# Graph attention over 2708 nodes: the last node tile's weights in four groups, and one division per block of four head pairs

## The chip, the cores and the metric

One core of one Trainium2 chip runs the whole program in one launch. The metric is the device time of an execution in microseconds (us), the median of several runs. A profile is one further execution, recorded by the hardware profiler, with its own time. TensorE is PE in the profile (its weight loads are PEld), VectorE is DVE, ScalarE is ACT, GpSimd is POOL, and SP issues most of the DMA transfers.

## The reference

Four graph layers work on x (2708 nodes, 512 features) and a 2708 x 2708 adjacency matrix; each is followed by a residual sum and a layer norm. Layers 0 and 1 are sums over neighbours, and the last stage is an attention with one head and a two-layer MLP. The change lies in the two attentions with eight heads of 64 features (layer 2, and the first half of layer 3), of this form:

```python
Wh = jnp.einsum('ni,hio->hno', h, W)
a1, a2 = (a[:, :OUT_F], a[:, OUT_F:])
f1 = jnp.einsum('hno,ho->hn', Wh, a1)
f2 = jnp.einsum('hno,ho->hn', Wh, a2)
e = jax.nn.leaky_relu(f1[:, :, None] + f2[:, None, :], ALPHA)
masked = jnp.where(adj[None] > 0, e, NEG_INF)
attention = jax.nn.softmax(masked, axis=-1)
h_prime = jnp.einsum('hnm,hmo->hno', attention, Wh)
```

## The kernel before, in words

**Tiles.** The nodes make NT = 22 tiles of P = 128 rows; the last tile (LAST) has only `few` = 20. The transposed mask `maskT` holds neighbours m on the partitions and nodes n on the columns. The columns are cut into two blocks of 11 tiles, 1408 and 1300 columns wide.

**Weights.** Up to factors that are applied elsewhere, the weight of neighbour m for node n is max(v[n], u[m]) times the mask, with v and u exponentials of the two projections f1 and f2. `Weights.weights` computes it for one neighbour tile j, one head and a whole block of columns in one DVE instruction, e (line 743). `Weights.load` broadcasts the head's row v to all partitions by DMA, `v_bc`. The column u of tile j is `ucol[:, j, h]`.

**Products and divisors.** PE multiplies e with R2, the projected features scaled by `ecol`, and sums over the tiles j into the PSUM tiles `po`, up to 512 columns each; the two heads of a pair use the two halves of PE's columns (line 937). For the softmax's divisor, `Weights.above` lets ACT compute c, which tells where u was above v (a steep sigmoid into 8 bits, line 770); PE multiplies c with the narrow columns `parts_c` into `pd` (`divisors`, line 839), and the mask with `parts_m` (`masks`, line 822). Each of these is a number split into three bf16 parts. `fold` adds the parts up by small matmuls (line 811), and `divide` makes reciprocals of the sums in `rcs` (lines 861 to 866).

**Order.** `heads_attention` goes through 8 runs per layer (two blocks, four head pairs each). In a run the 22 tiles j come in the order 0 to 9, LAST, 10 to 20, and at each tile the two heads' e, c and products. Steps that are left over from the run before are hung on positions of the order in `todo`: the rest of the divisors at 0, `fold` at 4, `divide` at 6, and in layer 2 turning the result (`turn`, `store`) at 8, 9, 12, 13, 16, 17. `keep` copies the mask's share of the divisors at position 2 of a block's first run. There are five buffers for e and three for `v_bc`. Each engine takes its instructions in one order that is fixed when the program is compiled.

**The last tile.** Its 20 neighbours would leave most partitions idle. So both heads of a pair share one e: rows 0 to 31 belong to the first head, rows 32 on to the second (TWIN = 32). `load_both` loads v for both (line 752), into the buffer that also holds the projection's weights, one run ahead. The mask rows of LAST lie four times on the partitions, at 0, 32, 64 and 96; the later two copies are made by two SP DMAs at line 585. In R2, `ecol` and `ucol` the rows of a head are zero for the other head.

**Projection.** `project` makes Wh for all tiles, with f1 and f2 as further columns of the same matmuls. On LAST with eight heads (`twice`) it copies the tile's 20 columns to a second place, and takes exponentials and scaled products head by head parity (lines 676 to 681). On the first block's and the last tile it splits `ecol` and the product of `ucol` and `ecol` into bf16 parts on DVE (`split`). The first few e's of an attention are computed while its projection still runs (`first`, `many` = 5 and 4), so that the attention's sixth e is the first that has to wait for a buffer. The sigmoids and the exponentials need different tables in ACT.

**After.** Layer 2's result goes to `o_dram` by SP; the next projection loads it through SP (`summed`). Layer 3's result goes to `oT_dram` and its reciprocals through `spread` to `rc_dram`, and the last projection loads both through SP (`elu_turned`).

Of the kernel before, what the change touches and what calls it, by code (L numbers as in the profile page):

```python
# [9 lines left out]
F32 = mybir.dt.float32  # L10
# [20 lines left out]
def kernel(  # L31
# [545 lines left out]
    for g in range(4):  # L577
        rows_m = ident[:, 32 * g:32 * g + 3 * H].rearrange("p (h i) -> p h i", i=3)
        rows_c = ident[:, 32 * g:32 * g + 12].rearrange("p (k q i) -> p k q i", k=2, q=2)
        nc.vector.tensor_reduce(pick_m[:, g], rows_m, AX.X, OP.add)  # L580
        nc.vector.tensor_reduce(pick_c[:, g], rows_c, AX.X, OP.add)


    for g in (2, 3):
        nc.sync.dma_start(maskT[g * TWIN:g * TWIN + few, LAST, :N], maskT[:few, LAST, :N])
# [20 lines left out]
    def project(name, source, layer, v_dram, cuts, turned=None, first=None):  # L606
# [12 lines left out]
        with ExitStack() as ph:  # L619
# [24 lines left out]
            for t in range(NT):  # L644
# [7 lines left out]
                twice = heads > 1 and t == LAST  # L652
                if twice:
                    nc.gpsimd.memset(xT[:, :, n:TWIN], 0.0)
                    nc.gpsimd.tensor_copy(xT[:, :, TWIN:TWIN + n], xT[:, :, :n])
                elif t == LAST:
                    for g in range(1, 4):
                        nc.gpsimd.memset(xT[:, :, g * TWIN - TWIN + n:g * TWIN], 0.0)
                        nc.gpsimd.tensor_copy(xT[:, :, g * TWIN:g * TWIN + n], xT[:, :, :n])
                m = n if t < LAST else TWIN + n if twice else 3 * TWIN + n  # L660
# [11 lines left out]
                if twice:  # L672
                    for k in range(2):
                        at = slice(k * TWIN, k * TWIN + n)
                        d2 = pm[1][at, D // 2 + k:D // 2 + heads:2]
                        nc.scalar.activation(ecol[at, t, k::2], d2, AF.Exp, scale=ALPHA)
                        for i in range(2):
                            nc.scalar.activation(ucol[at, t, i::2], d2, AF.Exp, scale=1.0 - ALPHA)
                        for a in range(2):
                            view = lambda y: y.rearrange("p (h k o) -> p h k o", k=2, o=HO)[:, :, k]  # L680
                            nc.vector.tensor_mul(view(R2[at, t, a * D // 2:(a + 1) * D // 2]), view(pm[a][at, :D // 2]),
                                                 ecol[at, t, a * hh + k:(a + 1) * hh:2, None].to_broadcast([n, hh // 2, HO]))
                else:
                    d2 = d if m == n else pm[1][:m, D // 2:D // 2 + heads]
                    nc.scalar.activation(ecol[:m, t, :heads], d2, AF.Exp, scale=ALPHA)
                    nc.scalar.activation(ucol[:m, t, :heads], d2, AF.Exp, scale=1.0 - ALPHA)
                with tc.issue_after(scaled[t - 1].ins) if first and t else nullcontext():
                    made = first(t) if first else None
                for a in range(0 if twice else 2):
                    to, src = R2[:m, t, a * D // 2:(a + 1) * D // 2], pm[a][:m, :D // 2]  # L690
                    if heads > 1:
                        with tc.issue_after(made.ins) if made else nullcontext():
                            scaled[t] = nc.vector.tensor_mul(to.rearrange("p (h o) -> p h o", h=hh),
                                                             src.rearrange("p (h o) -> p h o", h=hh),
                                                             ecol[:n, t, a * hh:(a + 1) * hh, None].to_broadcast([n, hh, HO]))
                    else:
                        scaled[t] = nc.scalar.activation(to, src, AF.Copy, scale=ecol[:m, t, 0:1])
                if heads > 1:
                    nc.scalar.activation(vcol[:n, t, :], b[:n, :], AF.Exp, scale=ALPHA - 1.0)
                    nc.gpsimd.tensor_scalar(bcol[:m, t, :], ucol[:m, t, :], -STEP * (1.0 + 2.0 ** -22), None,  # L700
                                            op0=OP.mult)
                a, z = next(c for c in cuts if c[0] <= t < c[1])
                if t == z - 1:
                    if heads > 1:
# [7 lines left out]
                        if z == NT:  # L712

                            nc.vector.tensor_copy(pairs_c[:, LAST, :, 0, 6:12], pairs_c[:, LAST, :, 1, 6:12])
# [8 lines left out]
    class Weights:  # L723
# [16 lines left out]
        def weights(self, b, h, j, v):  # L740
            c0, w = self.blocks[b][0] * P, self.width(b)
# [5 lines left out]
        def load_both(self, b, h0):  # L747
# [3 lines left out]
            for h, a, z in ((h0, 0, TWIN), (h0 + 1, TWIN, P)):  # L751
                nc.sync.dma_start(v[a:z, :w], self.v_dram[h, c0:c0 + w].partition_broadcast(z - a))
# [738 lines left out]
```

## Time and profile before

| what | us |
|---|---|
| median of 3 runs | 2942.97 (2942.67 to 2946.18) |
| the profiled execution | 2939.28 |
| its span, first to last instruction | 2937.5 |
| layers 0 and 1, to the first attention's projection | 858 |
| projection of layer 2 | 858.0 to 949.8 |
| attention of layer 2 | 949.8 to 1493.0 |
| projection of layer 3 | 1493.0 to 1596.0 |
| attention of layer 3 | 1596.0 to 2140.0 |
| last projection, last attention, MLP | 2140.0 to 2937.5 |

Over the whole span PE is busy 97%, PEld 54%, DVE 68%, ACT 52% and POOL 7%, and the granted TensorE clock is 0.995. A share of the whole span hides that the stages have different limits, so the busy times are best read stage by stage, and then the waits: the engine that others wait for sets the pace. A matmul's end is modelled in the profile, so a busy PE is not a PE at its peak. A fp32 matmul is recorded as two instructions.

### The profile page before, as it was taken

To read this page: it belongs to the slowest core of one execution; us is meant where nothing else is said; L and a number is where in the kernel's file an instruction comes from. 1 tells how busy PE (TensorE), PEld (TensorE's weight loads), DVE (VectorE), ACT (ScalarE), POOL (GpSimd) and SP (SyncE) were. 2 spreads that over 40 slices of the span, in tenths; PEclk is the share of its full clock that TensorE was granted. 3 is DMA by queue.
4 is the path that set the end of the run, shared out by engine and by line. 5 is a ranking of instruction groups with operands and counts; after the bars stand their busy time and mean duration, and the time that the engine had idled before them with its cause. 6 is when DMAs were issued, how large, how long until landed. Compare 5 with 4: busy or idle time off the path is not lost. (4 is left out here: it accounts for less than half of the span.)

```text
span 2937.5 us, 36437 instructions
## 1 busy us (share of the span) xinstructions
PE 2854.5 (97%) x14354; PEld 1590.3 (54%) x14354; DVE 1996.9 (68%) x2409; ACT 1515.0 (52%) x1761; POOL 220.2 (7%) x375
## 2 busy tenths in 40 slices
PE   8999999999999999999999999999999999999997
PEld 4557766458887333444466433444475555555555
DVE  6866637443234999999977999999953435445242
ACT  3546532123323999999965999999951000000001
POOL 1111101101110000000022000000000000000000
PEclk9999999999999999999999999999999999999999
DMA  5633326322222011111143111121061000000000
GB/s 131 129 87 76 104 79 192 113 67 91 81 74 82 30 40 39 38 45 48 32 151 123 40 40 39 43 64 37 33 158 61 4 26 15 25 15 16 15 22 21
DMA packets 121886, 185.71 MB, mean 63 GB/s; under 512 B 42455, under 2 KB 67276, under 8 KB 121706
## 3 DMA queue, kind: packets, MB, share of 16 engines
q1 hardware_dynamic: 91838, 121.62, 13.8%
q0 software_dynamic: 18864, 57.45, 6.9%
q10 hardware_dynamic: 11004, 4.22, 0.6%
q8 instruction: 115, 1.88, 0.3%
q14 instruction: 65, 0.53, 0.1%
HBM read 153.10 MB, written 44.65 MB: 67 GB/s over the span
## 5 line engine op out<-in xcount | busy, mean ns | idle before, releaser
L743 DVE SCALAR_TENSOR_TENSOR e<-v_bc,ucol,maskT 128x1408 f32<-128x1408 f32 (+3 forms) x804 | 1135.9, 1468 | 326.9 <-PE pn L1119 313.4
L770 ACT ACTIVATE c<-e,bcol 128x1300 fp8e4<-128x1300 f32 (+1 forms) x688 | 965.5, 1422 | 65.3 <-DVE e L743 22.3
L937 PE MATMUL po<-e,R 128*64 128x512 f32 (+2 forms) x4224 | 907.5, 549 | 30.4 <-DVE e L743 27.4
L937 PEld LDWEIGHTS po<-e,R 128*64 128x64 f32 x4224 | 341.9, 137 | 563.0 <-issue 386.1
L1119 PE MATMUL pn<-e,R 128*128 128x512 f32 (+3 forms) x1056 | 403.0, 545 | 1.1 <-DVE lin L1139 0.3
L1119 PEld LDWEIGHTS pn<-e,R 128*128 128x128 f32 (+1 forms) x1056 | 183.9, 190 | 197.1 <-issue 181.5
L1069 ACT ACTIVATE w<-pl,b 128x256 f32<-128x256 f32 (+1 forms) x88 | 41.0, 466 | 371.2 <-PE pl L1067 371.2
L496 PE MATMUL acc<-yH,kT 128*128 128x512 f32 x484 | 195.2, 409 | 4.6 <-ACT kT L369 4.5
L547 PE MATMUL acc<-yH,mf 128*128 128x512 f32 x484 | 185.0, 389 | 0.0
L496 PE MATMUL acc<-yL,kT 128*128 128x512 f32 x462 | 180.7, 391 | 0.0
L547 PE MATMUL acc<-yL,mf 128*128 128x512 f32 x462 | 179.7, 389 | 0.0
L663 PE MATMUL pm<-w,xT 128*128 128x264 f32 (+1 forms) x704 | 165.3, 387 | 2.0 <-ACT xT L135 1.1
L259 PE MATMUL pm<-weight,xT 128*128 128x512 f32 (+1 forms) x344 | 158.4, 603 | 8.1 <-DVE u L352 6.8
L1067 PE MATMUL pl<-lin 128*128 128x256 f32 (+1 forms) x704 | 156.1, 376 | 3.4 <-DVE lin L966 3.4
L122 POOL TENSOR_TENSOR ln_rs<-ln_rs,half 128x1 f32<-128x1 f32 (+1 forms) x88 | 53.5, 608 | 1407.7 <-DVE ln_rs L121 1358.2
L1092 PE MATMUL pl<-lin,w 128*128 128x512 f32 x336 | 150.8, 593 | 0.0
L1067 PEld LDWEIGHTS pl<-lin 128*128 128x128 f32 x704 | 131.3, 193 | 34.6 <-issue 15.8
L544 ACT CAST mf<-maskT 128x1024 fp32r<-128x1024 fp8e4 (+1 forms) x66 | 64.5, 978 | 151.7 <-PE acc L547 148.1
L663 PEld LDWEIGHTS pm<-w,xT 128*128 128x128 f32 (+1 forms) x704 | 127.9, 187 | 26.2 <-issue 2.9
L259 PE MATMUL pm<-w,xT 128*128 128x512 f32 x296 | 133.6, 594 | 5.3 <-ACT xT L135 2.1
L369 ACT ACTIVATE kT<-maskT 128x512 fp32r<-128x512 fp8e4 (+1 forms) x132 | 77.5, 594 | 115.5 <-PE acc L496 114.3
L839 PE MATMUL pd<-c,parts_c 128*12 128x384 fp8e4 (+2 forms) x2752 | 128.3, 307 | 0.0
(247 smaller groups left out, 2643.2 us busy)
## 6 DMA issues: line engine op xcount, KB each, us to landing
rows<-x_dram SPq DMA_DIRECT2D x63, 256.0 KB
v_bc<-v_dram SPq DMA_DIRECT2D x16, 704.0 KB
rows<-in_x_dram SPq DMA_DIRECT2D x42, 256.0 KB
x_dram<-u POOLq DMA_DIRECT2D x42, 256.0 KB, 2.6
v_bc<-v_dram SPq DMA_DIRECT2D x16, 650.0 KB
m<-in_adj_dram POOLq DMA_DIRECT2D x13, 677.0 KB, 7.0
r_dram<-u POOLq DMA_DIRECT2D x21, 256.0 KB, 2.4
rows<-r_dram SPq DMA_DIRECT2D x21, 256.0 KB
```

The costliest lines, as they stand in the source:

```text
L259: order(nc.tensor.matmul(pm[:m], xT[:, k, :m], w[:, k, :], start=(k == 0), stop=(k == KD - 1)))
L369: made = nc.scalar.activation(kT[:, :w], maskT[:, j, b[0] * P:b[0] * P + w], AF.Relu, scale=-1.0)
L496: nc.tensor.matmul(pa[t], kT[:, (t - b[0]) * P:(t - b[0] + 1) * P], y[:, j, :], start=(j == 0 and y is yH), stop=(j == LAST))
L547: nc.tensor.matmul(pa, mf[:, j - g0, :], y[:, j, :], start=(j == 0 and y is yH), stop=(j == LAST))
L663: nc.tensor.matmul(pm[a][:m, :D // 2 + heads], xT[:, k, :m], w[:, k, a, :D // 2 + heads], start=(k == 0), stop=(k == KD - 1))
L743: self.made = nc.vector.scalar_tensor_tensor(e[:, :w], v[:, :w], ucol[:, j, h:h + 1], maskT[:, j, c0:c0 + w], op0=OP.max, op1=OP.mult)
L770: nc.scalar.activation(c[:, :w], e[:, :w], AF.Sigmoid, bias=bcol[:, j, h:h + 1], scale=STEP, saturate=False)
L839: pe(nc.tensor.matmul(p[32 * g:32 * g + 12, :c1 - c0], parts_c[:, j, h, :], c[:, c0:c1], start=(i == 0 and h == hs[0]), stop=(i == NT - 1 ...
L937: pe(nc.tensor.matmul(po[i][HO * k:HO * k + HO, :c1 - c0], R2[:, j, h * HO:(h + 1) * HO], e[:, c0:c1], start=(i_ == 0), stop=(i_ == NT - 1)))
L1067: nc.tensor.matmul(pl[:, :w], self.lin1[:, k, f * P:(f + 1) * P], h[:, k, :w], start=(k == 0), stop=(k == KD - 1))
L1092: nc.tensor.matmul(pl[:n], gT[:, f, (t - t0) * P:(t - t0) * P + n], self.lin2[:, f, :], start=(f == 0), stop=(f == KF - 1))
L1119: nc.tensor.matmul(pn[k][:, :w], R2[at, j, k * P:(k + 1) * P], e[at, :w], start=(j == 0), stop=(j == NT - 1))
```

## The change

Three things are done.

First, LAST's weights in the head attentions are made for four groups of 32 rows: two heads by two segments of the block's columns. The second segment begins 512 columns (SEG) after the first, so an e holds 896 columns (or 788) in place of 1408 (or 1300). PE takes the product of each head and column part from the 32 rows of its group. `load_both` issues four DMAs, one for each group. The mask rows of the third and fourth group are shifted by 512 columns, and set back before the last projection (`last_rows`). The projection copies LAST to all four groups, treats all heads at once, and zeroes what does not belong to a group by a product with `sel` and by a copy within `ucol`.

Second, the sums of a block's four pairs are folded into one PSUM tile, `sums`, where they stay; `divide` runs once per block for all eight heads, with four instructions in place of five, and `keep` is gone. The buffers of `ps_t` go from two to one to make room in PSUM.

Third, what follows from this: divisors of LAST are cut at the segment's border, and the last projection uses the same copies as the others.

```diff
-    for g in (2, 3):
-        nc.sync.dma_start(maskT[g * TWIN:g * TWIN + few, LAST, :N], maskT[:few, LAST, :N])
+    def last_rows(cuts, skip):
+        for g in (2, 3):
+            for a, z in cuts:
+                c0, c1 = a * P, min(z * P, N)
+                nc.sync.dma_start(maskT[g * TWIN:g * TWIN + few, LAST, c0:c1 - skip], maskT[:few, LAST, c0 + skip:c1])
+    last_rows(blocks, SEG)
+    sel = late.tile([P, 2, 12], BF16, name="sel")
+    nc.gpsimd.memset(sel, 0.0)
+    for g in range(4):
+        nc.gpsimd.memset(sel[g * TWIN:(g + 1) * TWIN, g // 2, 6 * (g % 2):6 * (g % 2) + 6], 1.0)
...
-                twice = heads > 1 and t == LAST
...
+                m = n
+                if t == LAST:
+                    m = 3 * TWIN + n
                     nc.gpsimd.memset(xT[:, :, n:TWIN], 0.0)
+                    nc.gpsimd.tensor_copy(xT[:, :, TWIN:2 * TWIN], xT[:, :, :TWIN])
+                    nc.gpsimd.tensor_copy(xT[:, :, 2 * TWIN:m], xT[:, :, :TWIN + n])
...
-                if twice:
-                    for k in range(2):
-                        at = slice(k * TWIN, k * TWIN + n)
-                        d2 = pm[1][at, D // 2 + k:D // 2 + heads:2]
-                        nc.scalar.activation(ecol[at, t, k::2], d2, AF.Exp, scale=ALPHA)
-                        for i in range(2):
-                            nc.scalar.activation(ucol[at, t, i::2], d2, AF.Exp, scale=1.0 - ALPHA)
...
+                d2 = d if m == n else pm[1][:m, D // 2:D // 2 + heads]
+                nc.scalar.activation(ecol[:m, t, :heads], d2, AF.Exp, scale=ALPHA)
+                nc.scalar.activation(ucol[:m, t, :heads], d2, AF.Exp, scale=1.0 - ALPHA)
...
+                    for g in (1, 3) if t == LAST else ():
+                        at = slice(g * TWIN, g * TWIN + n)
+                        nc.gpsimd.tensor_copy(ucol[at, t, 0::2], ucol[at, t, 1::2])
...
+                            nc.vector.tensor_copy(at_last[:, :, 1, 0:6], at_last[:, :, 0, 0:6])
+                            nc.vector.tensor_mul(at_last.rearrange("p q k c -> p q (k c)"),
+                                                 at_last.rearrange("p q k c -> p q (k c)"),
+                                                 sel.rearrange("p k c -> p (k c)")[:, None, :].to_broadcast([P, H // 2, 24]))
+                            for a_, z_ in ((TWIN, 2 * TWIN), (2 * TWIN, P)):
+                                nc.gpsimd.memset(parts_m[a_:z_, LAST], 0.0)
...
-            for h, a, z in ((h0, 0, TWIN), (h0 + 1, TWIN, P)):
-                nc.sync.dma_start(v[a:z, :w], self.v_dram[h, c0:c0 + w].partition_broadcast(z - a))
+            for g in range(4):
+                a = c0 + SEG * (g // 2)
+                nc.sync.dma_start(v[g * TWIN:(g + 1) * TWIN, :w - SEG],
+                                  self.v_dram[h0 + g % 2, a:a + w - SEG].partition_broadcast(TWIN))
...
-            ps_t = ph.enter_context(tc.tile_pool(name=f"{name}_pt", bufs=2, space=PSUM))
+            ps_t = ph.enter_context(tc.tile_pool(name=f"{name}_pt", bufs=1, space=PSUM))
+            ps_s = ph.enter_context(tc.tile_pool(name=f"{name}_ps", bufs=1, space=PSUM))
...
-                    rc = sm.tile([P, 2, 12], F32, name="rc")
...
-                    nc.vector.tensor_add(by, by, sums[:, :, :, :, 0])
-                    nc.vector.tensor_add(rc, rc, r)
-                    nc.vector.tensor_scalar(rc, rc, 1e-30, None, op0=OP.max)
-                    nc.vector.reciprocal(r, rc)
+                    rc = sm.tile([P, 12 * H], F32, name="rc", bufs=1)
+                    by = rc.rearrange("p (t g h) -> p t g h", t=3, g=4)
+                    nc.vector.tensor_mul(by, of_c[:, :, :, 1], vcol[:, t0:t0 + 12].rearrange("p (g t) h -> p t g h", g=4))
+                    nc.vector.tensor_add(by, by, of_c[:, :, :, 0])
+                    nc.vector.scalar_tensor_tensor(rc, rc, 1e-30, of_m[:, b].rearrange("p t g h -> p (t g h)"),
+                                                   op0=OP.max, op1=OP.add)
+                    nc.vector.reciprocal(rcs[:, b].rearrange("p h (g t) -> p t g h", g=4), by)
...
-                steps = {0: [rest], 4: [fold], 6: [divide]}
+                steps = {0: [rest], 4: [fold], 6: [divide] if h0 == H - 2 else []}
...
-                        es = [att.weights(b, h0, j, both)] * 2
-                        cs = [att.above(b, h0, j, es[0])] * 2
+                        es = [att.weights(b, h0, j, both, SEG)] * 2
+                        cs = [att.above(b, h0, j, es[0], SEG)] * 2
...
-                            pe(nc.tensor.matmul(po[i][HO * k:HO * k + HO, :c1 - c0], R2[:, j, h * HO:(h + 1) * HO],
-                                                e[:, c0:c1], start=(i_ == 0), stop=(i_ == NT - 1)))
+                            at, a = slice(0, P), c0
+                            if j == LAST:
+                                s_ = int(c0 >= SEG)
+                                at, a = slice(TWIN * (2 * s_ + k), TWIN * (2 * s_ + k + 1)), c0 - SEG * s_
+                            pe(nc.tensor.matmul(po[i][HO * k:HO * k + HO, :c1 - c0], R2[at, j, h * HO:(h + 1) * HO],
+                                                e[at, a:a + c1 - c0], start=(i_ == 0), stop=(i_ == NT - 1)))
...
     lin = ph4.enter_context(tc.tile_pool(name="lin", bufs=1)).tile([P, KD * FF + KF * D + KD * 512], F32, name="lin")
+    last_rows([(0, NT)], 0)
     scaled = project("p4", None, 2, vd[2], quads, elu_turned)
```

## The prediction

> **What bounds the kernel now.** Only the two head attentions (layers 2 and 3) and their edges are touched, so I read the busy times by stage first:
>
> ```profile
> 949.80:1493.00 543.20, 531.80 (x3773) 221.38 (x3775) 534.80 (x410) 506.79 (x404) 3.62 (x3) 1.00 0.12 40
> 1596.00:2140.00 544.00, 526.66 (x3697) 220.51 (x3699) 535.23 (x410) 507.33 (x391) 5.53 (x9) 1.00 0.13 41
> ```
>
> The columns are the stretch, its length, PE, PEld, DVE, ACT and POOL busy, clock, DMA. DVE is busy 98.4% of both attentions. PE shows 98% and 97%, but its ends are modelled, so the waits must decide. In one run of a head pair (1111.7 to 1181.6) the table of waits gives PE and its weight loads 1.6 + 8.4 us waiting for DVE's e, and ACT 1.6 us. DVE's own waits over all of layer 2's attention are:
>
> ```profile
> DVE e L743 <- DMA v_bc<-v_dram: 2.9, 4, 0.8
> DVE e L743 <- ACT c L770: 2.6, 1, 2.6
> ...
> DVE e L743 <- PE po L937: 1.1, 2, 0.7
> ```
>
> So DVE is late and the others wait for it: what is taken off DVE inside an attention comes off the end. Durations are not prices here, because neighbouring DVE instructions overlap; the DVE timeline gives the pitch:
>
> ```profile
> 1028.92 12.85 DVE L743 SCALAR_TENSOR_TENSOR e<-v_bc,ucol,maskT 128x1408 f32<-128x1408 f32 x8
> 1041.68 0.19 DVE L861 TENSOR_TENSOR rc<-ps_t,vcol 128x24 f32<-128x24 f32 x1
> 1041.77 1.68 DVE L743 SCALAR_TENSOR_TENSOR e<-v_bc,ucol,maskT 128x1408 f32<-128x1408 f32 x1
> 1043.37 0.19 DVE L863 TENSOR_TENSOR rc<-rc,ps_t 128x24 f32<-128x24 f32 x1
> 1043.47 1.68 DVE L743 SCALAR_TENSOR_TENSOR e<-v_bc,ucol,maskT 128x1408 f32<-128x1408 f32 x1
> ```
>
> Eight e's span 12.85 us and one lasts 1.68, so the pitch is (12.85 - 1.68)/7 = 1.596 us; a small divide step between two e's adds only about 0.09. Last, the groups by shape, for the slopes:
>
> ```profile
> L743 DVE SCALAR_TENSOR_TENSOR e<-v_bc,ucol,maskT 128x1408 f32<-128x1408 f32 x336 | 542.2, 1677 | 11.7 <-ACT c L770 5.2 <-DMA v_bc<-v_dram 4.2 <-PE po L937 2.4
> L743 DVE SCALAR_TENSOR_TENSOR e<-v_bc,ucol,maskT 128x1300 f32<-128x1300 f32 x336 | 502.8, 1565 | 1.4 <-DMA v_bc<-v_dram 1.4
> ...
> L1043 DVE RECIPROCAL rc<-den 128x512 f32<-128x512 f32 x5 | 16.7, 3346 | 0.0
> ...
> L866 DVE RECIPROCAL rcs<-rc 128x24 f32<-128x24 f32 x16 | 4.8, 298 | 0.1
> ...
> L831 DVE COPY rcs<-ps_t 128x96 f32<-128x96 f32 x4 | 1.3, 326 | 0.1
> ```
>
> **A. The last node tile's weights, 512 columns narrower.** There are 16 runs (2 layers, 2 blocks, 4 pairs), each with one such e. The pitch is 1.596 at 1408 columns and 1.483 at 1300 (23 e's span 34.20 us and one lasts 1.57), so 1.04 ns per column, as the durations say too (112/108), and 512 columns are 0.53 us. 16 x 0.53 = **-8.5 us**. ACT loses 512 x 0.84 = 0.43 us per run (1468 against 1377 ns), hidden since ACT waits for DVE.
>
> **B. Dividing once per block.** From 1041.77 to 1048.64 four e's (6.38 us) and the divide's later steps take 6.87; with the first step one divide costs 0.57. Seven of eight per layer fall inside the attention (the eighth comes after the last e): 14 x 0.57 = 8.0. The four keeps cost 0.17 to 0.29 in pitch: 0.9. After it, only block 0's divide of each layer lies inside: three steps of 96 elements at 0.16 (24 elements cost 0.09, 72 more about 0.07), and a reciprocal. That one goes by element: 3346 ns at 512 and 298 at 24 make 6.25 ns each, so 96 elements take 0.2 + 72 x 0.00625 = 0.65. Together 1.13, twice 2.3. 8.9 - 2.3 = **-6.6 us**. The end divides grow from 1.2 to about 1.5 us: layer 2's lies before a DVE step that waits for ACT until 1499.2, layer 3's feeds reciprocals that only tiles 11 and later read. I count 0, at most +0.3 each.
>
> **C. The start of each attention.** Before, the second head's exponentials of the last tile sit behind the first sigmoid on ACT, with a table load each way:
>
> ```profile
> 1598.79 1.28 ACT L676 ACT_TABLE_LOAD   x1
> ...
> 1600.38 1.28 ACT L770 ACT_TABLE_LOAD   x1
> ...
> 1598.81 1.69 DVE L743 SCALAR_TENSOR_TENSOR e<-v_bc,ucol,maskT 128x1408 f32<-128x1408 f32 x1 [2.52 <-ACT c L770]
> 1600.52 0.48 DVE L681 TENSOR_TENSOR R<-pm,ecol 20x128 f32<-20x128 f32 x2
> ...
> 1604.21 1.67 DVE L743 SCALAR_TENSOR_TENSOR e<-v_bc,ucol,maskT 128x1408 f32<-128x1408 f32 x1
> ```
>
> DVE stands 2.52 us because its sixth e needs a buffer that the first sigmoid frees. Only then come the second head's R products (0.48) and the splits and memsets (about 3.2 us). After the change all heads take one exponential each for ecol and ucol, so these two table loads go, and both R products (0.76 for two wide ones) can run at once in the hole, with part of the splits. The first sigmoid ends some 0.3 us earlier, near 1598.5. Two POOL copies of ucol (0.25 each, as the POOL copies of xT) come in front of the splits: ready near 1596.2. DVE has R products and sums until 1596.9, then 1.6 us of splits, e, the other 1.6 and 0.25 for two new small products and copies: next e near 1602.0 against 1604.21. That is -2.2. If the compiled order leaves the splits behind the e, only 0.5 is left; if the hole fills wholly, -2.5. I take -2.0 per layer, **-4.0 us**. The Trainium skill ("ScalarE: Activation LUTs", What ACT_TABLE_LOAD costs) prices a switch at 2.66 us with its drain; here the sigmoid starts 1.3 us after the load begins. By the page ACT would win 5.3 us, by the trace 2.6; the sum stays, since DVE's hole caps it.
>
> **D. One PSUM buffer less for the turns.** Inside a run a turn follows the copy that frees its buffer by three node tiles, some 9.6 us: free. After layer 2's last pair three turns come together (1496.39) and then alternate with ACT copies: the last o_dram store, and SP's loads of o queued behind it (1500.40), come later by one turn (0.65). PE waits for those tiles, so **+0.6 us** (0 to 0.7).
>
> **E. PE.** Per run the last tile's products use a quarter of the rows, and divisors grow from 4 to 5 matmuls (under 0.1 us). The nearest row is the final attention's row-tiled group, 32*128: 40 records in 5.7 us, 0.14 each, against 373.4/840 = 0.44 for the full ones, so four tiles run together. The skill speaks against it ("TensorEngine Tiling (Array Packing)", Tiling Modes, Key Properties): changing the tiling mode drains TensorE, and each run now has two more changes. It gives no price; the row contains its changes of mode and is still three times faster. By the row PE gains about 1 us per run, by the rule it loses something; PE's 10 us of waiting covers either, so 0. Without cover, 1 us of drain per run would be +16.
>
> **F. Costed at nothing, with the cover.** load_both issues four DMAs for two: 0.32 us more each on SP, next used a run later; behind it wait stores and v loads due tens of us later (without cover, 32 x 0.32 = 10 us). The first mask copies: four issues at 0.82 end by 856.0, SP's next is at 857.82. Five POOL memsets (0.14 each) delay the clearing of ecol to 862.7; ACT first writes it at 864.0. The mask copies ahead of the last projection must wait for readers of the mask: even if that is DVE's last e (2138.0), two issues end at 2139.7, before SP's next at 2142.08 (without cover +1.7, since that stage waits for DMA). The projection's extra POOL copy ends near 942.2, PE needs it at 944.9.
>
> **Sum.** -8.5 - 6.6 - 4.0 + 0.6 = -18.5. The profiled execution took 2939.28 (span 2937.5 and 1.8 around it), so 2920.8; the median of the runs lies 3.7 higher, 2942.97, giving **2924.5 us**. This measurement can tell about 0.2%, 5.9 us, from no change.
>
> **The rivals.** *R0*, as above: 0.72, own range 2921 to 2929. *R1, DVE shrinks but the start hole stays* (order on DVE or a wait on POOL's copies): A, B, D and 0.5 per layer, -15.5: 2927.5. Speaking for it: the order is fixed at compile time and I can't see it. 0.18. *R2, a hidden wait takes half*: v_bc loads and e buffers already stop DVE up to 1 us in some runs; 0.6 us in each of 16 gives 2934. Against: ACT and PE have more slack than the 1 us per run removed. 0.05; another 0.02 that such waits take nearly all of it. *R3, slower: row tiles on PE.* If the last tile's products ran one by one with drains, PE would fall behind, and DVE stop for want of an e buffer. Today they take 12/4224 of 907.5 us, 2.6. PE must lose three e's of lead (4.8) and then 24.4/16 = 1.5 us per run before the total is 5.9 us worse: nearly 9 us for that step. Then 2949 or more. The 32*128 row speaks against. 0.03.
>
> Faster by over 0.2%: 0.95; within: 0.02; slower: 0.03. The range 2919 to 2932 takes in R0 with C at its bounds, B at 5.5 to 7, D at 0, the scatter of the runs, and R1.
>
> **What would show it.** Right: 16 e's from w at about 1.15 (896 columns) and 1.04 us (788); no table load at the projection's exponentials, DVE's wait for c before its sixth e well under 2 us; four reciprocals of 96 elements near 0.75; attentions near 535 us; DVE still 98% busy. Wrong: new DVE waits for PE's po or POOL, SP's o loads over 1 us late at layer 2's end, or the last projection starting late behind the mask copies.

## The result

The changed kernel takes 2924.30 us, the median of four runs (2921.44 to 2926.44), against 2943.66 for the kernel before (2942.67 to 2946.18): a ratio of 0.9933, with a 95% interval of 0.9918 to 0.9948, so 19.4 us less. 2924.5 was predicted. Two later sets of five runs gave 2924.46 and 2928.47, beside 2943.29 and 2944.30 for the kernel before; all fourteen runs have a median of 2925.2.

The profiled execution of the changed kernel took 2926.44 us (span 2924.5), the slowest of its four; that of the kernel before, 2939.28 (span 2937.5), lies below all its runs. So the pair of profiles shows only 13.0 us, and I compare stages, not spans. Executions of one kernel differ by 2 to 5 us in places that the change doesn't touch: in three executions of the changed kernel the last tile of layer 2's projection reaches DVE at 948.76, 950.45 and 953.61 us.

**The profile after.** First the busy times by stage, of the two attentions (stretch, length, PE, PEld, DVE, ACT and POOL busy, clock, DMA share, GB/s):

```profile
950.20:1480.00 529.80, 519.59 (x3724) 214.98 (x3726) 522.76 (x378) 494.85 (x397) 5.84 (x9) 1.00 0.12 38
1583.00:2123.00 540.00, 524.78 (x3723) 220.41 (x3724) 531.02 (x391) 500.17 (x398) 26.80 (x17) 1.00 0.11 38
```

DVE is busy 98.7% and 98.3%, as before: the bound has not moved. (The stretches are cut at other places than those of before, so their lengths don't compare.) Now DVE's groups by shape (count | busy us, mean ns | idle before):

```profile
L752 DVE SCALAR_TENSOR_TENSOR e<-w,ucol,maskT 128x896 f32<-128x896 f32 x8 | 9.2, 1150 | 0.0
...
L752 DVE SCALAR_TENSOR_TENSOR e<-w,ucol,maskT 128x788 f32<-128x788 f32 x8 | 8.3, 1043 | 0.0
...
L878 DVE RECIPROCAL rcs<-rc 128x96 f32<-128x96 f32 x4 | 3.0, 754 | 0.1
```

These are the sixteen narrow e's, 1150 and 1043 ns, and the four reciprocals, 754 ns: the sizes that the prediction named. The divide between the e's of block 1 (DVE's timeline: start, duration):

```profile
1246.05 0.25 DVE L874 TENSOR_TENSOR rc<-sums,vcol 128x96 f32<-128x96 f32 x1
...
1250.99 0.75 DVE L878 RECIPROCAL rcs<-rc 128x96 f32<-128x96 f32 x1
1251.65 1.48 DVE L752 SCALAR_TENSOR_TENSOR e<-v_bc,ucol,maskT 128x1300 f32<-128x1300 f32 x1
```

From the first step to the e behind the last are 5.60 us, in which three e's of 1.483 lie: 1.15 us for the divide, 1.13 predicted by the same count. The start of layer 3's attention, on DVE and then on ACT:

```profile
1590.10 0.15 DVE L681 TENSOR_SCALAR b<-pm 20x8 f32<-20x8 f32 x1 [1.96 <-PE pm L674]
...
1591.01 0.76 DVE L692 TENSOR_TENSOR R<-pm,ecol 116x256 f32<-116x256 f32 x2
...
1594.16 0.25 DVE L618 CAST parts_m<-rest 128x88 bf16<-128x88 f32 x1
1594.34 1.69 DVE L752 SCALAR_TENSOR_TENSOR e<-v_bc,ucol,maskT 128x1408 f32<-128x1408 f32 x1
...
1596.34 1.67 DVE L752 SCALAR_TENSOR_TENSOR e<-v_bc,ucol,maskT 128x1408 f32<-128x1408 f32 x1
```

```profile
1591.54 1.28 ACT L781 ACT_TABLE_LOAD   x1
...
1592.84 8.27 ACT L781 ACTIVATE c<-e,bcol 128x1408 fp8e4<-128x1408 f32 x6
```

One table load instead of three, and no idle time at all before the sixth e (1594.34), which still starts as the first sigmoid ends: the hole of 2.52 us is full. The gain shows one e later. The seventh e comes 6.24 us after the last tile's b (1590.10); before it was 1604.21 - 1594.47 = 9.74. Layer 2 has 6.34 against 9.87.

### The profile page after: what moved, and what is told of

The parts are those of the page before. It is cut to its first block, busy times and chain, and to the rows that moved or that the text cites. A ratio compares the mean times of both kernels' runs of the same rounds, so it can differ in the third digit from the quotient of the medians.

```text
span 2924.5 us, 36470 instructions
## 1 busy us (share of the span) xinstructions
PE 2842.8 (97%) x14370; PEld 1584.3 (54%) x14370; DVE 1983.5 (68%) x2341; ACT 1499.8 (51%) x1749; POOL 244.8 (8%) x387
## 5 line engine op out<-in xcount | busy, mean ns | idle before, releaser
L781 ACT ACTIVATE c<-e,bcol 128x1300 fp8e4<-128x1300 f32 (+2 forms) x688 | 956.6, 1412 | 63.4 <-DVE e L752 18.6
L953 PE MATMUL po<-e,R 128*64 128x512 f32 (+3 forms) x4224 | 894.7, 548 | 26.3 <-DVE e L752 24.3
L953 PEld LDWEIGHTS po<-e,R 128*64 128x64 f32 (+1 forms) x4224 | 333.4, 136 | 554.7 <-issue 390.4
L1083 PEld LDWEIGHTS pl<-lin 128*128 128x128 f32 x704 | 131.2, 193 | 34.5 <-issue 15.8
L544 ACT CAST mf<-maskT 128x1024 fp32r<-128x1024 fp8e4 (+1 forms) x66 | 64.5, 978 | 151.7 <-PE acc L547 148.1
```

The lines of the kernel that those rows point to most:

```text
L781: nc.scalar.activation(c[:, :w], e[:, :w], AF.Sigmoid, bias=bcol[:, j, h:h + 1], scale=STEP, saturate=False)
L953: pe(nc.tensor.matmul(po[i][HO * k:HO * k + HO, :c1 - c0], R2[at, j, h * HO:(h + 1) * HO], e[at, a:a + c1 - c0], start=(i_ == 0), stop=(i_ ...
L1083: nc.tensor.matmul(pl[:, :w], self.lin1[:, k, f * P:(f + 1) * P], h[:, k, :w], start=(k == 0), stop=(k == KD - 1))
```

## A ruler inside the attention

Differences of a few us drown in the spread of the whole. The e's of the last tile, one per run of a head pair, make a finer ruler: two of them lie one run apart. Here are the second and third of block 1 in layer 2, of the kernel before, of the two half changes (below), and of the changed kernel:

```profile
1326.16 1.57 DVE L743 SCALAR_TENSOR_TENSOR e<-w,ucol,maskT 128x1300 f32<-128x1300 f32 x1
...
1391.63 1.56 DVE L743 SCALAR_TENSOR_TENSOR e<-w,ucol,maskT 128x1300 f32<-128x1300 f32 x1
```

```profile
1322.25 1.03 DVE L752 SCALAR_TENSOR_TENSOR e<-w,ucol,maskT 128x788 f32<-128x788 f32 x1
...
1387.18 1.04 DVE L752 SCALAR_TENSOR_TENSOR e<-w,ucol,maskT 128x788 f32<-128x788 f32 x1
```

```profile
1327.38 1.56 DVE L743 SCALAR_TENSOR_TENSOR e<-w,ucol,maskT 128x1300 f32<-128x1300 f32 x1
...
1392.36 1.56 DVE L743 SCALAR_TENSOR_TENSOR e<-w,ucol,maskT 128x1300 f32<-128x1300 f32 x1
```

```profile
1321.14 1.04 DVE L752 SCALAR_TENSOR_TENSOR e<-w,ucol,maskT 128x788 f32<-128x788 f32 x1
...
1386.46 1.03 DVE L752 SCALAR_TENSOR_TENSOR e<-w,ucol,maskT 128x788 f32<-128x788 f32 x1
```

65.47 before, 64.93 with the groups alone (-0.54), 64.98 with the single divide alone (-0.49), and 65.32 in the changed kernel, where both should give 64.44. In layer 3 the changed kernel does show it (64.45, 64.52, 64.45). So in layer 2 something takes about 0.9 us of this run back. The whole ruler, worked out from such lines (the start is from the last tile's b to the first narrow e; us, layer 2 / layer 3):

| kernel | start | seven distances | of them block 1's three, each |
|---|---|---|---|
| before | 33.17 / 33.04 | 475.5 / 475.4 | 65.3 to 65.5 / 65.5 |
| groups only | 29.83 / 29.74 | 472.7 / 471.4 | 64.8 to 64.9 / 64.9 to 65.0 |
| divide once only | 33.16 / 33.03 | 473.4 / 472.9 | 64.8 to 65.0 / 65.0 to 65.1 |
| start only | 30.32 / 30.60 | 476.6 / 475.5 | 65.3 to 65.5 / 65.5 |
| changed | 29.81 / 29.72 | 472.9 / 468.6 | 65.0 to 65.3 / 64.5 |
| changed, norms held back | 29.84 / 29.74 | 469.1 / 468.1 | 64.3 to 64.5 / 64.5 |

## The experiments

**1. The four groups without the single divide.**

```diff
-            ps_t = ph.enter_context(tc.tile_pool(name=f"{name}_pt", bufs=1, space=PSUM))
-            ps_s = ph.enter_context(tc.tile_pool(name=f"{name}_ps", bufs=1, space=PSUM))
+            ps_t = ph.enter_context(tc.tile_pool(name=f"{name}_pt", bufs=2, space=PSUM))
...
-                steps = {0: [rest], 4: [fold], 6: [divide] if h0 == H - 2 else []}
+                steps = {0: [rest], 4: [fold], 6: [divide]}
...
-            todo = {12: products[:1], 16: products[1:2], 20: products[2:], NT: [fold]}
+            todo = {12: products[:1], 16: products[1:2], 20: products[2:], NT: [fold], NT + 2: [keep]}
```

`fold`, `keep` and `divide` are those of the kernel before.

> The changed kernel with the old divide: one divide per pair, the keeps and two buffers for the turns are back; the four groups of the last 20 nodes stay, and with them the joint start of each attention. Theory 1 (DVE time inside an attention counts in full, and the start is worth 3.5 us per layer, as the trace of the changed kernel shows by the sixth e): -8.5 - 7.0 = -15.5 us against the kernel before. Theory 2 (the prediction's size of the start, 2.0 per layer): -12.5. Theory 3 (hidden waits for loads and buffers give half of DVE's saving back): about -11, with DVE waiting for v_bc or e buffers 4 us longer than before in the two attentions. The sixth e's distance from the last projected tile should be about 6.3 us (9.8 before) in theories 1 and 3.

Measured: 2926.77 us (2926.47 to 2930.58) against 2944.35, ratio 0.9944 (0.9930 to 0.9957), -17.6 us. By the ruler the narrow e is worth 0.54 us per run, 16 x 0.54 = 8.6, and the start 3.3 in each layer. DVE's waits for v_bc and PE's po are 5.1 us in layer 2 and 3.7 in layer 3, against 4.0 and 3.8 before: theory 3's extra 4 us are not there. Theory 1 stands; the total is 2 us above it, within the spread.

**2. The single divide without the groups**, the same edit the other way round, in the kernel before.

> The kernel before with the divide of a block's four pairs made once (and so one buffer for the turns); the last 20 nodes keep their two groups. Theory 1: -6.6 for the steps on DVE and +0.6 for the turns, so -6.0 us, with every pair but the one that divides 0.57 us shorter. Theory 2 (the one buffer for the turns costs more than one turn, since the loads of o wait for it): -4, and the first o load of layer 3 comes 2 us or more later behind layer 2's last e. Theory 3 (hidden waits take half): -3.

Measured: 2938.57 us (2934.97 to 2939.88), ratio 0.9978 (0.9967 to 0.9988), -5.8 us, close to theory 1's -6.0; but the ruler shows less. On it a run without a divide is 0.48 us shorter, not 0.57, and the run with the block's divide is 0.7 us longer in layer 3 (68.62 against 67.93). The seven distances lose 2.1 and 2.5 us. The first three o loads are issued 8.96, 10.39 and 10.78 us behind layer 2's last e, where they were at 9.26, 9.65 and 10.15, so theory 2's delay of 2 us of the first load is not there.

**3. The start alone.** In the kernel before, the exponentials of both heads ahead of all R products:

```diff
                     for k in range(2):
                         ...
                         for i in range(2):
                             nc.scalar.activation(ucol[at, t, i::2], d2, AF.Exp, scale=1.0 - ALPHA)
+                    for k in range(2):
+                        at = slice(k * TWIN, k * TWIN + n)
                         for a in range(2):
                             ...
                             nc.vector.tensor_mul(view(R2[...]), view(pm[a][at, :D // 2]), ...)
```

> The kernel before, with one edit at the last tile of each projection: the exponentials of both heads of a pair are issued before the first product for R, so that no sigmoid comes between them. Two table loads of ScalarE go in each of layers 2 and 3. Theory 1 (the start is what the change gained there): the sixth e comes 3 to 3.5 us earlier in each layer, -6 to -7 us. Theory 2 (the prediction's size): -2.0 per layer, -4.0 us. Theory 3 (the start gains nothing that lasts, since PE or the first sigmoids are late next): within 1 us of the kernel before.

Measured: 2940.08 us (21 runs, 2934.56 to 2942.42), ratio 0.9982 (0.9976 to 0.9989): -4.3 us by the medians, -5.3 by the ratio. ACT's timeline at layer 3's start has the exponentials together and one table load:

```profile
1598.83 0.21 ACT L678 ACTIVATE ucol<-pm 20x4 f32<-20x4 f32 x2
...
1599.26 1.28 ACT L772 ACT_TABLE_LOAD   x1
...
1600.55 9.62 ACT L772 ACTIVATE c<-e,bcol 128x1408 fp8e4<-128x1408 f32 x7
```

The ruler's start is 2.85 and 2.44 us shorter, 5.3 in all. The seven distances of layer 2 give 1.1 us of it back, mostly a longer wait for v_bc at its change of block (1.30 against 0.62 us); layer 3's give back nothing (475.5 against 475.4). So most of what the change gains at the start is not the wider tile but the order of six small ACT instructions. It lies between the two theories. Of the changed kernel's further 0.5 and 0.9 us, the two wide R products make about 0.4: from start to next start they hold DVE for 0.67 us, the four narrow ones here for 1.05. I did not trace the rest.

**4. The narrow e on GpSimd.**

```diff
-                        es = [att.weights(b, h0, j, both, SEG)] * 2
+                        es = [att.on_pool(b, h0, j, both, SEG)] * 2
...
+        def on_pool(self, b, h, j, v, skip):
+            c0, w = self.blocks[b][0] * P, self.width(b) - skip
+            nc.gpsimd.tensor_scalar(v[:, :w], v[:, :w], ucol[:, j, h:h + 1], None, op0=OP.max)
+            nc.gpsimd.tensor_tensor(v[:, :w], v[:, :w], maskT[:, j, c0:c0 + w], OP.mult)
```

> The changed kernel with the narrow e of the last tile moved from DVE to GpSimd, which writes it in place over its v in two steps (maximum with ucol, then times the mask). DVE loses 8 x 1.07 + 8 x 0.95 = 16 us. Theory 1 (DVE bounds and GpSimd is free): -16 us against the changed kernel, so about -35 against the kernel before. Rival (GpSimd is held off while DVE works back to back): in the changed kernel's trace a GpSimd copy of 128 x 8 elements that starts at 2089.60 beside fourteen e's takes 21.0 us and ends just after DVE's chain of e's does, against 1.48 us for the same copy in the kernel before. Then the last tile's e is not ready until DVE runs out of e buffers and stops: three or more e's of standstill per run, 16 x 3 us or more, and the kernel is slower than the changed one by 20 us or more.

Measured: 2942.98 us (13 runs, 2938.47 to 2944.87), ratio to before 0.9994 (0.9985 to 1.0002): 18.7 us slower than the changed kernel. The size is near the rival's, the mechanism is only half of it. Here is one run, GpSimd's two steps and then the two e's of DVE that met them, and below it GpSimd's first step in a later run with the e's beside it:

```profile
1060.05 4.88 POOL L758 TENSOR_SCALAR w<-w,ucol 128x896 f32<-128x896 f32 x1 [60.86 <-PE po L959]
1065.02 3.12 POOL L759 TENSOR_TENSOR w<-w,maskT 128x896 f32<-128x896 f32 x1
```

```profile
1062.55 2.35 DVE L752 SCALAR_TENSOR_TENSOR e<-v_bc,ucol,maskT 128x1408 f32<-128x1408 f32 x1
...
1066.42 3.21 DVE L752 SCALAR_TENSOR_TENSOR e<-v_bc,ucol,maskT 128x1408 f32<-128x1408 f32 x1
```

```profile
1707.87 29.97 POOL L758 TENSOR_SCALAR w<-w,ucol 128x896 f32<-128x896 f32 x1 [34.56 <-DMA w<-v_dram]
```

```profile
1705.06 30.40 DVE L752 SCALAR_TENSOR_TENSOR e<-v_bc,ucol,maskT 128x1408 f32<-128x1408 f32 x19
1736.12 9.60 DVE L752 SCALAR_TENSOR_TENSOR e<-v_bc,ucol,maskT 128x1408 f32<-128x1408 f32 x5 [0.66 <-DMA v_bc<-v_dram]
```

GpSimd is held off, as the rival said: the maximum takes 2.53 to 8.88 us in fourteen runs and 29.97 and 30.06 in two, there until just behind a pause of DVE (0.66 us, before 1736.12). But DVE does not stand for want of buffers. It waits for GpSimd in its turn: the two e's shown take 2.35 and 3.21 us instead of 1.68, 2.2 us more together, and those around them keep 1.68. The second of them starts within GpSimd's product, which ends at 1068.14, and ends 1.49 us after that, almost a whole e later. In all sixteen runs an e ends 1.37 us (1300 columns) or 1.48 to 1.49 us (1408) after the product does. In the two attentions 27 e's are longer than their like, by 28 us in all; the e's saved are 16 us, and DVE stands idle 3.3 us longer than in the changed kernel's profile. That makes 15 us, and from the last tile's b to the last e the two layers are 16.0 us longer. The Trainium skill ("SBUF — State Buffer", Who interferes with whom) says that a DVE instruction with two SBUF inputs contends with a GpSimd instruction that reads SBUF; e reads v and the mask. The trace agrees, and here an e waits until GpSimd's whole product is over, not for a share of it.

**5 and 6. The changed kernel again, and with two layer norms held back.** Where did the ruler's 0.9 us in layer 2 go? DVE's timeline of the changed kernel in that stretch:

```profile
1421.67 0.18 DVE L119 BATCH_NORM_AGGREGATE ln_mv<-ln_st 128x2 f32<-128x6 f32 x1
1421.88 0.15 DVE L121 TENSOR_SCALAR ln_rs<-ln_mv 128x1 f32<-128x1 f32 x1
1422.79 0.16 DVE L126 SCALAR_TENSOR_TENSOR ln_mv<-ln_mv,ln_rs 128x1 f32<-128x1 f32 x1 [0.75 <-POOL ln_rs L122]
1423.25 7.51 DVE L752 SCALAR_TENSOR_TENSOR e<-v_bc,ucol,maskT 128x1300 f32<-128x1300 f32 x5 [0.30 <-ACT c L781]
```

Layer norms of layer 3's first two node tiles lie between layer 2's e's, and one of them makes DVE wait 0.75 us for GpSimd, with every e queued behind it. The compiled order put twelve of their steps there. Seven of these lie between the e's in the kernel before too; the changed kernel adds five and the wait. To see what they cost, all twelve were held back:

```diff
     def summed(sm, t, n):
-        nc.vector.tensor_mul(by_head, by_head, rcs[...])
+        with tc.issue_after(lasts[0].ins) if t < 2 else nullcontext():
+            nc.vector.tensor_mul(by_head, by_head, rcs[...])
```

Here `lasts[0]` is layer 2's last e.

> The changed kernel once more, unedited, to tell its time more closely than four runs do, and to see which of its waits come again. Theory 1 (the parts add up, and the distances between the last tile's e's tell what each is worth): -7.5 for the narrow e (-8.5 by the prediction), -5 for the divide, -6.7 for the starts, so -19 to -20 us against the kernel before. Theory 2 (the parts measured alone, -17.6 and -5.8, add up): -23 us. The 2.3 us wait of DVE for v_bc at layer 2's change of block: by theory 1 a late transfer of one execution, under 1.2 us here; if the change makes it, again near 2.3. The three layer-2 runs with layer norms between their e's (65.13, 65.32, 64.98 us against 64.45 in layer 3) should be the same to 0.2 us, since the order is fixed.

> The changed kernel with one edit: the first step of the layer norms of node tiles 0 and 1 for layer 3 may be issued only behind layer 2's last e, where the order of the kernel before had most of that work. Theory 1 (between the e's that work costs DVE what it takes, and behind them it lies in DVE's wait for o): the three last runs of layer 2 come to 64.45 us as in layer 3, and 2 us come off the whole: -2 us against the changed kernel. Rival (it is only moved): the attention is 2 us shorter and layer 3's projection 2 us longer, 0 against the changed kernel.

Measured: the changed kernel 2924.46 (ratio 0.9939, 0.9926 to 0.9953), so -18.8 us, theory 1's size and not theory 2's; norms held back 2921.03 (2919.66 to 2923.74; ratio 0.9926, 0.9912 to 0.9939). The three distances are 65.13, 65.31 and 65.23 us again in the first, and 64.34, 64.35 and 64.52 in the second. So these norms cost the attention 2.2 to 2.6 us, taking three executions of the changed kernel and two with the norms held back. Their steps and waits are longer than that, but without them DVE waits for v_bc once in each of the three runs, 0.75 to 1.19 us, where the kernel before does not wait at all:

```profile
1356.08 28.27 DVE L752 SCALAR_TENSOR_TENSOR e<-v_bc,ucol,maskT 128x1300 f32<-128x1300 f32 x19 [0.92 <-DMA v_bc<-v_dram]
```

So the expectation was wrong that the kernel before had most of this work behind the attention: holding it back also takes out what that kernel pays. Whether some of it comes back later is less clear: from layer 2's last narrow e to the next projection's last b it is 138.1 us in the first and 138.8 in the second, and 137.5 to 142.3 over all the executions of experiments 1 to 8 that keep the e's on DVE, the kernel before included. DVE's wait at layer 2's change of block, 2.30 us in the first profile of the changed kernel, is 0.74 in the second and 1.71 in the third. It is 0.62 in the kernel before and 1.27 to 1.35 in the three partial changes, so this wait has another length each time, and the change isn't shown to cause it.

> norms_held_back once more, unedited, beside the next kernel: 2921 us, or 22 to 23 us below the kernel before, if its 3.4 us under the changed kernel are no accident; 2924 if they are.

Measured: 2923.78 us (2922.94 to 2926.49), ratio 0.9933 (0.9919 to 0.9946), 21.6 us below the kernel before by the medians, 19.7 by the ratio. Ten runs with the norms held back have a median of 2923.2, fourteen of the changed kernel 2925.2. The ruler shows the 2 us each time (64.29, 64.18, 64.60 here), but this execution has 140.5 us up to the projection's last b, against 138.1 to 138.7 in three executions of the changed kernel. So up to 2 us may be moved, not saved, and the totals don't decide it.

**7. Loads of v one e earlier.** At each run's end the first head's last e goes ahead of the second head's last but one, so that its v buffer is free sooner; norms held back as well.

```diff
+                        elif i_ == NT - 2:
+                            es = [att.weights(b, hs[0], j, vs[0])]
+                            held = att.weights(b, hs[0], order[-1], vs[0])
+                            es.append(att.weights(b, hs[1], j, vs[1]))
```

> As norms_held_back, and at the end of each pair's run the first head's e of the last tile is made before the second head's e of the tile ahead of it, so that the v buffer that the next pair's second load waits for is free one e (1.5 to 1.6 us) sooner. Theory 1 (DVE waits at the start of a run because that load lands late): DVE's waits for v_bc, 3.6 us in the two attentions and 2.3 more at the change of block, go nearly to nothing: -4 us against norms_held_back. Rival (PE's po, which lacks one e for longer at each end of a run, or the e buffers stop DVE instead): the v_bc waits go and waits for PE po or ACT of the same size come, 0 against norms_held_back or slower.

> norms_held_v_early with its second edit kept only for the three runs of each layer in which it made the distance between the last tile's e's shorter each time: the runs of block 1 except the last (63.76, 63.78, 63.76 us in layer 2 and 63.70, 63.69 in layer 3, against 64.34, 64.35, 64.52 and 64.45, 64.52 in norms_held_back). Theory 1 (there the late v load was what DVE waited for, and the losses of norms_held_v_early lie in block 0, where PE's po stopped DVE up to 1.6 us, and behind layer 3's last e): the end of layer 3 and the last projection are as in norms_held_back, and 6 x 0.6 = 3.6 us come off: -3.6 against norms_held_back. Rival (the order of the steps behind layer 3's last run changes with the edit whatever the run): the last projection starts 3 us or more later again, and the kernel is no faster than norms_held_back.

> v_early_three_runs with one more edit: the eight loads of the last projection's weights go through SyncE's queue instead of ScalarE's. In v_early_three_runs the compiled order put them behind ScalarE's last sigmoid, so that they were issued at 2127.98 and later (in the changed kernel from 2089.83 to 2112), PE's first product of the last projection waited for them, and DVE stood 10.84 us. Theory 1 (that order was the whole of the loss): the weights are loaded inside layer 3's last run again, DVE's wait before the last projection's b goes back under 1 us, and what is left is the gain of the earlier v loads: 3 to 4 us below norms_held_back and norms_held_again, 2918 to 2920 us. Rival (more was moved by the edit than these loads, as DVE's steps for tile 2 that now lie among the last e's): 2922 us or more.

Measured: 2928.05 (ratio 0.9947, 0.9934 to 0.9961), 2930.02 (0.9950, 0.9936 to 0.9963) and 2925.69 us (0.9942, 0.9928 to 0.9955). In block 1 the waits for v do vanish, and the distances fall to 63.7 to 63.8 us (layer 3's last to 64.3); in the first kernel waits for PE's po (up to 1.6 us) take their place in block 0. The other two leave block 0 as it was, but in both DVE waits 2.6 us for v_bc in one run of layer 3 (distance 70.8, against 68.9 with the norms held back). And the second of these kernels has this on DVE and on ACT's queue, behind layer 3's attention:

```profile
2142.38 0.16 DVE L681 TENSOR_SCALAR b<-pm 128x1 f32<-128x1 f32 x1 [10.84 <-PE pm L674]
```

```profile
2127.98 0.37 ACTq L631 DMA_DIRECT2D w<-in_L_gnn_Wo_dram  x1
```

The edit touches no such load, yet the compiled order now has the last projection's weights behind ACT's last sigmoid, and PE and DVE wait for them (DVE 7.97 us in the first kernel, where six of the eight loads come behind it). With these loads on SyncE's queue the 10.84 us wait is 0.71 again, but steps of tile 2's layer-3 result still lie among the last e's (the last e ends 37.7 us after the last narrow one, not 34.6). So the rivals' outcome held each time, in part by mechanisms that they didn't name, and no version of this edit beats norms held back.

**8. PE's last tile over all rows.**

```diff
-                                at, a = slice(TWIN * (2 * s_ + k), TWIN * (2 * s_ + k + 1)), c0 - SEG * s_
+                                a = c0 - SEG * s_
```

> The changed kernel with PE's products of the last tile taken over all 128 rows again instead of 32 of them, so that no tile of rows is used there and no mode changes in an attention for them. The sums then run over all four groups of rows, which the output is not meant to hold: only the time is read. Theory 1 (the row tiles run side by side, PE waits for DVE anyway): PE's group with the last tile takes about 9.7 instead of 9.1 us and the time is the same, within 1.5 us of the changed kernel. Rival (changes of mode drain PE and the row tiles run one by one): the group gets shorter than 9.1 us, and if PE's lag ever stops DVE the kernel gets faster by 1 us or more.

Measured: 2927.24 us (2922.59 to 2928.51), 2.8 us above the changed kernel, with intervals that overlap (0.9943, 0.9929 to 0.9956). PE's group with the last tile, first of the changed kernel, then of this one:

```profile
1188.53 9.12 PE L953 MATMUL po<-e,R 128*64 128x512 f32 x48
```

```profile
1188.83 9.67 PE L953 MATMUL po<-e,R 128*64 128x512 f32 x48
```

The row tiles are 0.55 us faster in this run, mode changes included, as theory 1 said. With all rows DVE waits for PE, ACT and DMA somewhat more in this one execution, so the difference in time may be real, but what the data tell is only that row tiles cost nothing.

> The changed kernel unedited beside the kernel above, on the same chip: 2924 to 2925 us, as twice before.

Measured: 2928.47 us (2921.26 to 2930.23), ratio 0.9940 (0.9927 to 0.9954).

## Why the prediction was right, point by point

- **A, narrower e's: right.** 8.5 predicted, 16 x 0.54 = 8.6 by the runs of block 1. (Over all distances the groups alone gain 7.9; the wait at layer 2's change of block was 0.65 us longer there.) DVE's time in an attention counts almost one to one: R2's 0.6 us of new waiting per run is not there in the half changes, where DVE's waits over all the distances grow by 0.9 and 0.6 us. (Experiment 6 shows a limit: where DVE's work hides a late v_bc, taking it out pays only in part.)
- **B, the single divide: mis-sized.** 6.6 predicted. The ruler gives 2.1 and 2.5 us, 4.6 in all. The term at fault is the price of one pair's divide. The prediction summed 0.57 up to the start of the e behind the reciprocal, but that e is a short one:

```profile
1048.64 1.58 DVE L743 SCALAR_TENSOR_TENSOR e<-v_bc,ucol,maskT 128x1408 f32<-128x1408 f32 x1
```

  It lasts 1.58 us instead of 1.68, so the e after it starts 0.09 early, and 0.48 is left, which is what a run loses on the ruler. The block's divide, 1.15 by the prediction's count, is 1.06 for the same reason. So the steps come to 14 x 0.48 + 0.9 - 2 x 1.06 = 5.5; 0.6 of the other 0.9 us are longer waits for v_bc and po in that execution, most of them at layer 2's change of block.
- **C, the start: mis-sized the other way.** 2.0 per layer predicted, bound 2.5; 3.3 to 3.4 came. The bound took the hole as the most that could be had. But between b and the seventh e DVE needs 6.24 - 1.69 = 4.55 us for what took 9.74 - 1.69 - 2.52 = 5.53 before, the hole left out. R's two wide products make 0.3 of this 1.0 (0.67 us for 0.96); the rest lies in the splits, memsets and sums, the same eighteen steps, which now come in one stretch; it was not traced further. Table loads went as forecast, 1.28 us each. The Trainium skill ("ScalarE: Activation LUTs", What ACT_TABLE_LOAD costs) adds a drain and comes to 2.66; the trace shows none, as the sigmoid starts at 1592.84, 0.02 us behind the load. It made no difference, as DVE's hole capped it.
- **D, one turn buffer less: seen in part.** The first o load is issued 8.66 us behind the last e instead of 9.26, the second and third 0.4 and 0.3 us later (0.7 and 0.6 with the single divide alone). +0.6 was predicted; what it costs is within the spread of that stage.
- **E and F, the hidden parts: right.** Row tiles take 0.14 us each (64 in 8.7 us, where 64 full-row ones take 17.7), and R3's one-by-one products do not occur. The last mask copies, feared for 2139.7, are issued at 2089.5 already.
- **Not foreseen, and paid:** five more steps of the two layer norms among layer 2's e's, with their waits (+2.1: the three distances of block 1 against layer 3's), which the order of the program caused, and a later start of the last projection. There the first product with the loaded result comes 13.9 to 14.3 us behind layer 3's last e in six executions of the changed kernel, of norms held back and of experiment 8, and 12.4 to 12.8 in the kernel before and in the three partial changes; the kernel before first, then the changed one:

```profile
2150.77 1.23 DVE L1011 TENSOR_TENSOR lin<-lin 128x1024 f32<-128x1024 f32 x1 [4.03 <-DMA lin<-rc_dram]
```

```profile
2136.92 1.23 DVE L1027 TENSOR_TENSOR lin<-lin 128x1024 f32<-128x1024 f32 x1 [5.26 <-DMA lin<-rc_dram]
```

  The loads are issued as early as before (4.05 us behind the last e), but DVE waits longer for them. Only kernels with both parts show it, and why is open.

By their steps the parts come to 8.6 + 5.5 + 6.7 = 20.8 us. The norms take 2.1 back, and the wait at layer 2's change of block is 1.0 us longer than in the kernel before on the average of three executions: 17.7 us. That is about what the attentions show directly. From the last tile's b to the last e, layer 2 takes 536.4, 535.2 and 535.7 us against 542.9, and layer 3 takes 533.0, 532.8 and 533.3 against 543.6: 7.1 and 10.5 us less. With about +1.4 for the last projection this makes -16 of the -19.4 measured (-18.8 and -15.8 in the later sets); the rest is within what executions differ by elsewhere. So 18.5 was close by luck in part: B's excess and C's shortfall cancelled, and the unforeseen losses were small. The two halves measured alone add up to -17.6 - 5.8 = -23.4, and with the norms held back the changed kernel comes to -22.3 and -21.6. The norms are a likely part of what it lacks to that sum, but a spread of 2 us in each number, and that holding back takes out more than the change put in, keep this from being shown.

## What to carry to other kernels

With one engine busy 98% of a stage, a narrower instruction on it paid its pitch here (0.54 us of 0.53 forecast), and a hole at a stage's start is worth as much as many narrow instructions: look for what a table switch or a small dependent step holds up, since reordering alone (six small ACT instructions here) may fill it. A bound on such a gain has to count the work around the hole too, not only the hole. A pitch that is read off a step between two instructions has to be followed one instruction further, until the old pitch is back. And after any edit compare the compiled order of the engines far from the edit: here it put more of two layer norms between the e's (2 us), and in two kernels of experiment 7 the next stage's weights behind the last sigmoid (waits of 8.0 and 10.8 us).

## What the hardware did that I had not expected

GpSimd and DVE make each other wait, and an average hides it: in experiment 4 most e's keep their length (1.68 us for 1408 columns), a few take up to 3.28, and GpSimd's maximum takes up to 30.06. It shows without that edit too. In all three profiles of the changed kernel one GpSimd copy of 128 x 8 elements takes 21.0 us beside fourteen e's (1.48 in the kernel before):

```profile
2089.60 21.04 POOL L632 COPY w<-wa 128x8 f32<-128x8 f32 x1 [26.52 <-DVE e L752]
```

```profile
2089.37 20.87 DVE L752 SCALAR_TENSOR_TENSOR e<-v_bc,ucol,maskT 128x1300 f32<-128x1300 f32 x14
2110.14 0.44 DVE L1029 TENSOR_SCALAR spare<-spare 128x512 f32<-128x512 f32 x1
```

This copy and its like at layer 2's end lie beside e's in all fourteen executions, and each time they end 0.05 to 0.10 us after a DVE instruction does: the first or second e (1.4 to 3.0 us), or only when a chain of e's is over (21.0, 27.8 and 32.7 us). So GpSimd is held off by DVE there. Why it gets its turn after one e in some executions and after a whole chain in others is open.
